# Regrouping the last expert layer of a fused transformer kernel, and the order of its row scatters

## Chip, cores and metric

The kernel runs on one core of a Trainium2 chip. The metric is device time in microseconds (us) of one execution; lower is better. A core has five engines that each work through their own queue of instructions in order: TensorE (PE) for matmuls, VectorE (DVE), ScalarE (ACT), GpSimd (POOL) and SyncE (SP), which here only issues DMAs. Engines wait for one another by semaphores. An instruction that waits also holds back whatever stands behind it in its queue.

## The reference

The input is 8 sequences of 512 tokens with 128 features. Six layers follow one another, each with a layer norm in front and a residual sum behind:

```python
x = x + 0.5 * moe(layernorm(x))    # 8 experts, each token goes to its best 2
x = x + attention(layernorm(x))    # 16 heads of 8, causal, rotary
x = x + 0.5 * moe(layernorm(x))    # same weights as the first
x = x + 0.5 * fp6(layernorm(x))    # quantized product, 128 x 128
x = x + mix(layernorm(x))          # gates, a scan along the tokens, gated FFN
x = x + 0.5 * fp6(layernorm(x))
```

An expert computes `relu(x @ W1 + b1) @ W2 + b2` with W1 of 128 x 512. The two chosen experts' outputs are weighted by a softmax over their two scores.

## The kernel before

All eight sequences X[0] to X[7] stay on chip. The layers are numbered by s: s = 0 and s = 2 are the two expert layers, s = 1 is attention, and the last three layers together are a "tail", one for each sequence.

**An expert layer** works on groups of sequences, from the table `GROUPS` (line 29): for s = 0 three and five, for s = 2 four and four. For a group, four things follow one another.

- The *front*, `moe_front` (line 330), normalizes each sequence into a tile (`um`, five buffers, for s = 2; the tiles `um` and `a0` to `a4` for s = 0) and computes the routing scores. It then finds each token's two experts and its place in a table of rows sorted by expert: the integers `at`, the gates `g1`, and the expert of each tile of rows, `eid` (lines 412 to 481). When that is done it enters the group in `groups`.
- The *scatters* (line 489) come next in the same generator: eight indirect DMAs for each sequence, issued by POOL, write its normalized rows into `rows_in[g]` in memory. So three, four and five sequences have 24, 32 and 40 scatters.
- The *tiles*, `moe_tiles` (line 498): `tiles_of(n)` = 4n + 7 tiles of 256 rows for n sequences, so 19, 23 and 27 for three, four and five. SP loads a tile's expert weights `wx` (line 511) and its rows `xs` (line 515) four tiles ahead. The load of the rows waits for all scatters of the group. PE transposes the rows (`xp`, line 525), multiplies by W1 (`hp`, line 539), ACT and DVE apply bias and relu (`hs`, lines 547 and 549), PE multiplies by W2 (`yp`, line 559), DVE adds the bias (`yo`) and SP stores to `rows_out[g]` (line 571). A tile is emitted in four pieces, each ending in a `yield`.
- The *combine*, `moe_combine` (line 595), gathers each token's two rows with indirect DMAs on POOL (`y`, line 623), eight for each sequence. DVE adds them, weighted, to X (line 614). When a sequence is through, (s, b) is in `done`.

`rows_in[g]` and `rows_out[g]` are as long as the longest group with that g needs: 23 tiles for g = 0 and 27 for g = 1. Each is cleared once at the start (line 162), ahead of the loads of the other constants on SP's queue.

**Attention** (line 639) runs through 32 units, four for each sequence. Its main loop has 212 half-steps, each a `yield`. It is emitted as a software pipeline in which the row maxima run four steps ahead of the exponentials, so its last half-steps hold exponentials and value products only.

**The tail** of a sequence (line 999) is fp6, mix, fp6 and a store: 27 short pieces, each of which crosses from one engine to another. `tails` (line 1007) keeps up to four alive; a new one may start every eight steps if its sequence is in `done`. One step of `tails` advances every live tail by one piece.

**The order of the work is written out by hand**: each engine's queue is filled in the order of emission. All parts are Python generators. `drive(main, (side, rate), ...)` (line 64) takes one step of the main generator and then `rate` steps, on average, of each side. `until(gen, ready)` runs a generator until a condition holds, checked after each `yield`; `behind` holds a generator back until a condition holds; `sent(s, g)` is true when all of a group's scatters are emitted and `filled(s, g)` when all of its tiles are stored. At the start of the program:

```python
finish(until(first_front, lambda: (0, 0) in groups))
finish(until(second_front, lambda: (0, 1) in groups))
finish(first_front)
finish(second_front)
```

The first `until` looks only when the generator yields, and the first `yield` after the entry in `groups` is the one behind the first scatter. So this order holds one scatter of the first group, then the second group's front with its first scatter, then the remaining 23 of the first group and 39 of the second.

Later, attention is the main generator (line 1055). Beside it run the remaining work of layer 0 (`early`, `tiles`, `gathering`), the front and scatters of s = 2's first group (`third`, one piece a half-step), its second group's front (`fourth`, held back until the first is sent) and the tiles of s = 2 (`beside`, held back likewise). After attention, the tiles of the first group run to their end (line 1060). Then the tiles of the second group are the main generator, with the combine of the first and the tails beside them (line 1062). At the end the remaining tails run with the combine of the second group (line 1063).

Of the kernel before, what the change touches and what calls it, by code (L numbers as in the profile page):

```python
# [25 lines left out]
NGF = 3  # L26
TW = 256

GROUPS = {0: [[0, 1, 2], [3, 4, 5, 6, 7]], 2: [[0, 1, 2, 3], [4, 5, 6, 7]]}
SIZES = sorted({len(g) for gs in GROUPS.values() for g in gs})  # L30
GTX = SIZES[-1] * NT


def tiles_of(n):

    return 2 * n * S // TW + NE - 1
# [27 lines left out]
def drive(main, *sides):  # L64

    due = [0.0] * len(sides)
    for _ in main:
        for i, (g, rate) in enumerate(sides):
            due[i] += rate
            while due[i] >= 1.0:  # L70
                due[i] -= 1.0
                next(g, None)
# [12 lines left out]
def kernel(  # L85
# [69 lines left out]
    for g in range(2):  # L155
        n = max(tiles_of(len(gs[g])) for gs in GROUPS.values()) * TW
        rows_in.append(dram.tile([n, P], F32, tag=f"rows_in{g}", name=f"rows_in{g}"))
# [140 lines left out]
    def data_from(ins, others):  # L298

        for o in others:  # L300
            tc.add_manual_dep(
                ins.ins, o.ins.name,
                mybir.DependencyInfo(mybir.DependencyClass.Sync, mybir.DependencyReason.DATA),
                reason="rows",
            )

    def unordered(ins, key):

        tc.declare_no_dep(ins.ins, group=key, reason="rows of their own")
        tc.add_to_no_dep_group(key, ins.ins)  # L310
        return ins

    def filled(s, g):
        return len(groups[s, g]["stored"]) == tiles_of(len(GROUPS[s][g]))

    def sent(s, g):
        return (s, g) in groups and len(groups[s, g]["scattered"]) == 2 * NT * len(GROUPS[s][g])

# [11 lines left out]
    def moe_front(s, g):  # L330

        name = f"{s}_{g}"
        bs = GROUPS[s][g]
        GT, NTL = len(bs) * NT, tiles_of(len(bs))
# [147 lines left out]

        scattered = []
        groups[s, g] = dict(at=at, gates=g1, eid=eid, scattered=scattered, stored=[])
        for n in range(len(bs)):
            for k in range(2):
                for t in range(NT):
                    i = n * NT + t
                    ins = nc.gpsimd.indirect_dma_start(  # L489
                        out=rows_in[g][0 : NTL * TW, :],  # L490
                        out_offset=bass.IndirectOffsetOnAxis(ap=at[:, k, i : i + 1], axis=0),
                        in_=us[n][:, t, :], in_offset=None,
                        bounds_check=NTL * TW - 1, oob_is_err=False,
                    )
                    scattered.append(unordered(ins, f"out{name}"))
                    yield

    def moe_tiles(s):

        order = [(g, i) for g in range(2) for i in range(tiles_of(len(GROUPS[s][g])))]  # L500
        T = {}
# [93 lines left out]
    def moe_combine(s, g):  # L595

        state = groups.pop((s, g))
        at, gates = state["at"], state["gates"]
        NTL = tiles_of(len(GROUPS[s][g]))
        assert len(state["stored"]) == NTL  # L600
        waiting = []

        def put():
            f, y, t, b = waiting.pop(0)
            f(y, t)
            if t == NT - 1:
                done.add((s, b))

        for n, b in enumerate(GROUPS[s][g]):

            def weighted(y, t, n=n, b=b):
                for k in range(2):
                    i = n * NT + t
                    nc.vector.scalar_tensor_tensor(
                        X[b][:, t, :], y[:, k, :], gates[:, k, i : i + 1], X[b][:, t, :],
                        ALU.mult, ALU.add,
                    )

            for t in range(NT):
                y = wk.tile([P, 2, P], F32, tag="y", name=f"y_{s}_{b}_{t}", bufs=6)  # L620
                for k in range(2):
                    i = n * NT + t
                    ins = nc.gpsimd.indirect_dma_start(  # L623
                        out=y[:, k, :], out_offset=None,
                        in_=rows_out[g][0 : NTL * TW, :],
                        in_offset=bass.IndirectOffsetOnAxis(ap=at[:, k, i : i + 1], axis=0),
                        bounds_check=NTL * TW - 1, oob_is_err=False,
                    )
                    data_from(ins, state["stored"])
                    yield  # L630
                waiting.append((weighted, y, t, b))
                if len(waiting) > 3:
                    put()
        while waiting:
            yield
            put()
# [370 lines left out]
    def tails(bs):  # L1007

        pend = list(bs)
        live = []  # L1010
        step = 8
        while pend or live:
            if pend and len(live) < 4 and step >= 8 and (2, pend[0]) in done:
                live.append(tail(pend.pop(0)))
                step = 0
            for g in list(live):
                if next(g, live) is live:
                    live.remove(g)
            step += 1
            yield  # L1020


    def behind(gen, ready):
        while not ready():
            yield
        yield from gen
# [7 lines left out]
    for s in GROUPS:  # L1034
        for g in range(2):
            fronts[s, g] = moe_front(s, g)
# [7 lines left out]
    tiles = moe_tiles(0)  # L1044
# [3 lines left out]
    early, late = moe_combine(0, 0), moe_combine(0, 1)  # L1048
    drive(until(tiles, lambda: (0, 1) in done), (early, 1.0), (fp6_weight(), 0.2))
    backlog += [early, tiles, late]  # L1050
    gathering = behind(late, lambda: filled(0, 1))
    third, fourth = fronts[2, 0], behind(fronts[2, 1], lambda: sent(2, 0))
    more_tiles = moe_tiles(2)
    beside = behind(more_tiles, lambda: sent(2, 0))
    drive(
        attention(list(range(nb)), 1),
        (early, 1.0), (tiles, 2.2), (gathering, 0.8), (third, 1.0), (fourth, 1.0), (beside, 0.9),
    )
    finish(third)
    drive(until(beside, lambda: filled(2, 0)), (fourth, 1.5))  # L1060
    rest = tails(GROUPS[2][0] + GROUPS[2][1])
    drive(beside, (fourth, 1.5), (moe_combine(2, 0), 1.0), (rest, 0.33))
    drive(rest, (moe_combine(2, 1), 2.0))


# [75 lines left out]
```

## Time and profile before

| | |
|---|---|
| median of 3 runs | 1178.27 us (1177.59 to 1180.08) |
| the profiled execution | 1177.05 us |
| its span in the profile | 1175.4 us |
| PE, DVE, ACT, POOL busy | 958.0, 688.2, 503.6, 540.3 us |
| attention's last output product (L801) begins | 749.2 us |
| first hp matmul (L539) of s = 2's second group | 818.1 us |
| last scan of a tail (L954) begins | 1133.17 us |

The profile is of one execution, with times in us from the start of the span. The page lists, for each engine, its busy time, then the span in 40 slices of 29.4 us with the busy share in tenths, and then groups of instructions: line, engine, operation, output <- input, count, busy time, mean duration in ns, and the idle time of the engine ahead of them with what ended it. The list of waits says which engine, at which line, waited for what: total, number of times, longest. The timeline has start, duration, engine, line, operation, count, and in brackets the idle time before it and its releaser. The windows give each engine's busy time within a stretch. PEld is PE's weight load, which overlaps PE. A matmul of these float32 operands shows in the trace as several passes.

### The profile page before, as it was taken

Reading aid. Unit: us, or ns where it says so; the run is one execution under the profiler, and the core shown is the slowest. Engines: PE = TensorE matmul, PEld = TensorE weight load, DVE = VectorE, ACT = ScalarE, POOL = GpSimd, SP = SyncE. Lnnn points to the kernel's source line nnn. Section 1 sums busy time; section 2 is a strip of 40 time slices with the busy share of each in tenths; the row PEclk is TensorE's granted clock in tenths of the full one; section 3 lists DMA queues with packets and bytes.
Section 4 is the critical chain, followed back from the end, with each engine's and each line's share of the span. In section 5 each row is a group of like instructions: output and inputs, shape, how many; then the busy total and the mean of one; then the engine's idle time right before and its main releaser. Section 6 shows DMA issues by size and latency. Waiting matters only on the chain.

```text
span 1175.4 us, 20511 instructions
## 1 busy us (share of the span) xinstructions
PE 958.0 (82%) x6809; PEld 654.6 (56%) x6809; DVE 688.2 (59%) x2532; ACT 503.6 (43%) x1095; POOL 540.3 (46%) x696
## 2 busy tenths in 40 slices
PE   3507997999999999999999899995969984466764
PEld 3407996777664444544445466784867852334432
DVE  7302334565567878777877563441466576777763
ACT  1302332344455655666465455331235553344441
POOL 2077707112147775433388422054572148664431
PEclk9999999999999999999999899997979995777777
DMA  9318977443200000000001422474755311100000
GB/s 290 119 50 273 272 234 220 128 143 114 73 24 26 24 24 13 1 2 2 1 31 53 140 64 84 145 228 146 232 157 164 105 32 29 33 25 10 9 9 18
DMA packets 88313, 110.07 MB, mean 94 GB/s; under 512 B 9360, under 2 KB 69648, under 8 KB 88208
## 3 DMA queue, kind: packets, MB, share of 16 engines
q1 hardware_dynamic: 80016, 91.97, 25.8%
q0 software_dynamic: 8192, 16.79, 4.7%
q8 instruction: 54, 0.88, 0.3%
q14 instruction: 51, 0.42, 0.1%
HBM read 79.63 MB, written 29.10 MB: 93 GB/s over the span
## 4 chain that ended last, share of the span: by engine, by line
PE 55%; DVE 18%; issue 11%; POOL 9%; ACT 3%; DMA 3%; POOLq 0%; SPq 0%; DVEq 0%; ACTq 0%
PE sa L705 11%; PE hp L539 9%; PE yp L559 9%; PE av L768 7%; DVE seen L722 3%; POOL y L623 3%; POOL rows_in L489 3%; PE sb L705 2%; DVE st L240 2%; PE gt L981 1%; PE tp_st L225 1%; PE lp L344 1%; PE up L982 1%; DMA rows_in<-um,at 1%; PE tp L225 1%
## 5 line engine op out<-in xcount | busy, mean ns | idle before, releaser
L722 DVE CUSTOM_DVE_ANT_0 seen<-sa,future_s 128x128 f32<-128x128 f32 (+3 forms) x512 | 224.7, 486 | 92.6 <-PE sb L705 87.6
L750 ACT ACTIVATE pm<-sb 128x512 f32<-128x512 f32 (+1 forms) x384 | 181.7, 523 | 143.6 <-PE sb L705 124.2
L547 ACT ACTIVATE hs<-hp,wx 128x256 f32<-128x256 f32 x276 | 119.9, 470 | 266.8 <-PE hp L539 254.2
L705 PE MATMUL sb<-qa,ka 32*128 32x512 f32 (+3 forms) x1024 | 210.2, 473 | 1.6 <-DVE nstat L722 1.5
L559 PE MATMUL yp<-wx,hs 128*128 128x128 f32 x1472 | 201.2, 281 | 4.8 <-ACT hs L547 3.4
L755 POOL TENSOR_SCALAR_AFFINE_SELECT pm<-pm 128x256 f32<-128x256 f32 x256 | 101.7, 411 | 220.4 <-ACT pm L750 218.0
L705 PE MATMUL sa<-ta_k,qm 32*128 32x384 f32 (+3 forms) x1024 | 200.5, 473 | 0.6 <-DVE nstat L722 0.4
L559 PEld LDWEIGHTS yp<-wx,hs 128*128 128x128 f32 x1472 | 190.4, 196 | 18.1 <-issue 6.9
L539 PE MATMUL hp<-xt,wx 128*128 128x256 f32 x736 | 197.8, 393 | 0.0
L623 POOL DMA_INDIRECT y<-rows_out,at x128 | 132.0, 1031 | 83.2 <-DMA rows_out<-yo 50.8
L549 DVE TENSOR_SCALAR hs<-hp,wx 128x256 f32<-128x256 f32 x92 | 44.4, 483 | 178.3 <-ACT hs L547 173.4
L539 PEld LDWEIGHTS hp<-xt,wx 128*128 128x128 f32 x736 | 131.0, 198 | 20.9 <-issue 5.9
L705 PEld LDWEIGHTS sa<-ta_k,qm 32*128 32x128 f32 x1024 | 91.4, 186 | 76.3 <-DVE nstat L722 20.2
L489 POOL DMA_INDIRECT rows_in<-um,at x88 | 87.1, 990 | 45.6 <-issue 19.6
L705 PEld LDWEIGHTS sb<-qa,ka 32*128 32x128 f32 x1024 | 99.7, 186 | 10.5 <-DVE nstat L722 4.2
L768 PE MATMUL av<-pm,vpad 128*32 128x512 f32 (+3 forms) x1024 | 92.3, 456 | 0.0
L525 PE MATMUL xp<-cst,xs 128*128 128x128 f32 x184 | 36.6, 282 | 60.3 <-DMA xs<-rows_in 60.3
L232 POOL TENSOR_TENSOR rs<-rs,mhalf 128x4 f32<-128x4 f32 x35 | 36.2, 1035 | 100.6 <-DVE rs L231 98.2
L527 DVE COPY xt<-xp 128x256 f32<-128x256 f32 x92 | 38.1, 414 | 54.0 <-PE xp L525 54.0
L251 ACT ACTIVATE um<-x,nb_um,rs 128x128 f32<-128x128 f32 x96 | 39.5, 482 | 67.3 <-DVE nb_um L248 59.4
L225 PE MATMUL tp_xd<-cst,q 128*128 128x128 f32 x64 | 15.1, 379 | 64.5 <-POOL q L884 64.5
L525 PEld LDWEIGHTS xp<-cst,xs 128*128 128x128 f32 x184 | 26.2, 145 | 70.9 <-issue 62.2
(190 smaller groups left out, 1367.7 us busy)
## 6 DMA issues: line engine op xcount, KB each, us to landing
wx<-in_wexp SPq DMA_DIRECT2D x92, 578.0 KB, 4.0
xs<-rows_in SPq DMA_DIRECT2D x92, 128.0 KB, 4.1
rows_out<-yo SPq DMA_DIRECT2D x92, 128.0 KB, 2.3
rows_in<-zero SPq DMA_DIRECT2D x1, 3456.0 KB, 25.3
rows_in<-zero SPq DMA_DIRECT2D x1, 2944.0 KB, 12.8
x<-in_x SPq DMA_DIRECT2D x8, 256.0 KB, 4.8
y<-rows_out,at POOLq DMA_INDIRECT x128
out_x<-x SPq DMA_DIRECT2D x8, 256.0 KB, 2.0
```

The lines of the kernel that those rows point to most:

```text
L489: ins = nc.gpsimd.indirect_dma_start(out=rows_in[g][0 : NTL * TW, :], out_offset=bass.IndirectOffsetOnAxis(ap=at[:, k, i : i + 1], axis=0) ...
L525: nc.tensor.transpose(xp[:, ts(h, P)], t["xs"][:, h, :], ident)
L539: nc.tensor.matmul(hp[:, k, :], wx[:, E_W1 + fc * P : E_W1 + (fc + 1) * P], t["xt"], start=True, stop=True,)
L547: nc.scalar.activation(hs[:, fc, :], hp[:, k, :], AF.Relu, bias=bias)
L549: nc.vector.tensor_scalar(hs[:, fc, :], hp[:, k, :], bias, 0.0, ALU.add, ALU.max)
L559: nc.tensor.matmul(yp[:, h, :], t["hs"][:, fc, ts(h, P)], wx[:, E_W2 + fc * P : E_W2 + (fc + 1) * P], start=(fc == 0), stop=(fc == NFC - 1),)
L623: ins = nc.gpsimd.indirect_dma_start(out=y[:, k, :], out_offset=None, in_=rows_out[g][0 : NTL * TW, :], in_offset=bass.IndirectOffsetOnAxi ...
L705: nc.tensor.matmul(sc[:, at : at + hi - lo], stat[rows, ts(m, P)], mov[rows, lo:hi], start=True, stop=stop,)
L722: nc.vector.tensor_tensor_reduce(out=seen(w), in0=sc[:, at : at + w], in1=future_s[:, S - w : S], scale=-1.0, scalar=3.0e38, op0=ALU.add, ...
L750: nc.scalar.activation(pm[:, h % 2, 0:w], sc[:, 0:w], AF.Exp, scale=scale)
L755: nc.gpsimd.affine_select(out=dg, in_=dg, pattern=[[0, 2], [1, P]], compare_op=ALU.is_ge, fill=0.0, base=0, channel_multiplier=-1,)
L768: nc.tensor.matmul(av[32 * j : 32 * j + 32, m * P :], Q[b]["v"][:, m * NH + NR * j + r, :], U[n]["pms"][p, j // 2][:, j % 2, at : at + S - ...
```

## The change

There are four edits. The layer s = 2 is grouped in five and three sequences. A `yield` stands between the entry in `groups` and the first scatter. The tiles of s = 2 advance beside attention at a rate of 2.0 instead of 0.9. The tails advance beside the second group's tiles at 0.6 instead of 0.33.

```diff
-GROUPS = {0: [[0, 1, 2], [3, 4, 5, 6, 7]], 2: [[0, 1, 2, 3], [4, 5, 6, 7]]}
+GROUPS = {0: [[0, 1, 2], [3, 4, 5, 6, 7]], 2: [[0, 1, 2, 3, 4], [5, 6, 7]]}
...
         groups[s, g] = dict(at=at, gates=g1, eid=eid, scattered=scattered, stored=[])
+        yield
         for n in range(len(bs)):
...
-        (early, 1.0), (tiles, 2.2), (gathering, 0.8), (third, 1.0), (fourth, 1.0), (beside, 0.9),
+        (early, 1.0), (tiles, 2.2), (gathering, 0.8), (third, 1.0), (fourth, 1.0), (beside, 2.0),
...
-    drive(beside, (fourth, 1.5), (moe_combine(2, 0), 1.0), (rest, 0.33))
+    drive(beside, (fourth, 1.5), (moe_combine(2, 0), 1.0), (rest, 0.6))
```

The lines below the new `yield` have numbers one higher in the changed kernel: the scatters of line 489 are at 490, the hp matmuls of 539 at 540. The text keeps the numbers of the kernel before. With the new groups, `rows_in[0]` has 27 tiles instead of 23, and the table of constants no longer holds a pattern for groups of four.

## The prediction

> **What bounds the kernel now.** The page comes first: its span, the slices of TensorE (PE) and the scatter row.
>
> ```profile
> span 1175.4 us, 20511 instructions
> PE   3507997999999999999999899995969984466764
> PEclk9999999999999999999999899997979995777777
> L489 POOL DMA_INDIRECT rows_in<-um,at x88 | 87.1, 990 | 45.6 <-issue 19.6
> ```
>
> One slice is 29.4 us. PE is full from slice 3 to about slice 32, so there only PE's work and the holes in it count; slices 0 to 2 and the last seven are bound by something else. Then the waits, the PE and POOL lists, name the holes (total, times, longest):
>
> ```profile
> PE tp_xd L225 <- POOL q L884: 64.5, 15, 13.8
> PE xp L525 <- DMA xs<-rows_in: 60.3, 5, 38.4
> POOL rows_in L489 <- DVE qs L463: 29.9, 1, 29.9
> ```
>
> PE waits 60.3 us for rows scattered by GpSimd (POOL). The timeline of the start shows why the longest of those is 38.4 us:
>
> ```profile
> 25.87 1.21 POOL L489 DMA_INDIRECT rows_in<-um,at  x1 [4.60 <-DVE q L461]
> 57.02 0.99 POOL L489 DMA_INDIRECT rows_in<-a,at  x1 [29.95 <-DVE qs L463]
> 86.55 0.98 POOL L489 DMA_INDIRECT rows_in<-um,at  x1 [0.30 <-issue]
> 87.83 0.98 POOL L489 DMA_INDIRECT rows_in<-a,at  x1 [0.30 <-issue]
> 88.81 0.38 SPq L515 DMA_DIRECT2D xs<-rows_in  x1
> 91.13 0.66 PE L525 MATMUL xp<-cst,xs 128*128 128x128 f32 x2 [38.39 <-DMA xs<-rows_in]
> ```
>
> One scatter of the first group (um) goes at 25.87. The next in POOL's queue is one of the second group (a), whose places are ready only at 57. The other 23 of the first group stand behind it, though their places are known since 25.87. A second hole lies late, before the tiles of the last layer's second group:
>
> ```profile
> 801.06 1.03 PE L539 MATMUL hp<-xt,wx 128*128 128x256 f32 x4
> 811.26 0.97 POOL L489 DMA_INDIRECT rows_in<-um,at  x1 [0.30 <-issue]
> 815.94 0.66 PE L525 MATMUL xp<-cst,xs 128*128 128x128 f32 x2 [13.85 <-DMA xs<-rows_in]
> ```
>
> The windows compare the stages (length, then busy PE, PEld, DVE, ACT, POOL; clock; DMA share; GB/s):
>
> ```profile
> 708.00:740.00 32.00, 30.19 (x245) 19.85 (x244) 10.70 (x45) 15.65 (x35) 7.59 (x17) 1.00 0.19 59
> 818.00:846.00 28.00, 28.00 (x193) 25.99 (x193) 10.85 (x34) 9.18 (x21) 12.18 (x13) 0.98 0.83 256
> 1004.00:1046.00 42.00, 23.37 (x101) 14.77 (x100) 32.45 (x95) 14.85 (x34) 29.84 (x28) 0.76 0.12 32
> 1050.00:1106.00 56.00, 39.75 (x144) 24.85 (x145) 40.48 (x130) 27.50 (x60) 25.22 (x23) 0.70 0.03 10
> ```
>
> The end of attention and the tiles alone fill PE. Where only tails run (the last two), VectorE (DVE) is the fullest, at 77% and 72%, and no engine is full: chains of short steps across engines set the pace.
>
> **What the Trainium skill says.** "DMA: Bandwidth & Descriptors", section on the anatomy of a DMA on the GpSimd path: each has a fixed cost of about 2 us. The trace agrees: scatters land 2.25 us after issue. "SBUF — State Buffer", section "SBUF: two separate sides": GpSimd can't write descriptors while a DVE operation holds the shared port. This matters because the first group's scatters will now run beside the routing of the second. The trace shows little of it: from 830 to 850, beside a half-busy DVE (9.71 of 20 us), gathers keep a spacing of 1.30 us, against 1.28 for scatters with DVE idle at 60 to 87. "TensorE: Matmul & The Clock Gate", section "Part 1: The HAM clock gate": after some 3.4 us of idleness PE starts at half clock. The trace agrees: after the 13.85 us hole eight yp matmuls take 1.92 us, later 1.05.
>
> **The change, part by part.**
>
> *The yield before the scatters.* POOL's order becomes 24 scatters of the first group, then 40 of the second. The places are there at 25.87. The clear that comes before grows from 2944 KB (12.8 us, issued at 7.68) to 3456 KB; in proportion 15.0 us, landing at 22.7, so still hidden. The constants lose the pattern for four sequences, an eighth of that load; at most 0.3 us, counted as nothing. The 24th scatter issues at 25.87 + 23 x 1.283 = 55.4, where now the last is at 86.55: **-31.1 us**. The steps that follow it (SP issue, load, first xp, 4.6 us) stay. The second group's 40 start at about 57 instead of 87.8 and so keep the same lead over its tiles. POOL, SP and PE all move together, up to the third layer's front. Bounds: -25 if descriptors are delayed by DVE (it is busy 11.5 us from 27 to 91; half of it), -32 at best.
>
> *Groups of five and three; rate 2.0 beside attention.* Before, about 9.5 tiles of the first group ran beside attention (38 of its 92 hp matmuls in program order, four to a tile). In the changed order, 40 scatters follow the fifth sequence at one per attention step, and the first xp stands after the last transpose of attention. So none runs inside attention; 4.5 precede the last sequence's y, but behind all of attention's scores. The rate of 2.0 has almost nothing to act on. PE's work is only moved, since PE is full there. Built up from PE's times:
> - y of the sixth sequence: 639.29 - 31.1 = 608.2.
> - The next y, with the same matmuls as from 590.12 to 639.29 and no tiles: +49.2 = 657.4.
> - The last stretch without tiles: attention's PE work from 708 to 740 is 9.5 + 5.6 + 2.6 us, and 3 for its chain of exponentials and copies: +20.7 = 678.
> - A new wait. Six scatters stand after the last mask: 6 x 1.28 + 2.25 landing + 3.6 to xp = 13.5 us, less some 4.5 of value matmuls: +9. First fill of the tile pipeline, as from 91.13 to 95.23: +4. Together 691. Now this start costs only 2.20 + 2.84 us. Bounds for both items together 5 to 20.
> - 27 tiles at 3.73 us (xp at 821.15, the next at 824.88): 100.7. The last y, three fronts with um transposes and scores, and the routing's matmuls: 8.5. Together **800**, against 818 now.
>
> The 13.85 us hole goes: the fronts of three need about 25 us after the last sequence (749 to 771.4 now, for the routing), then 24 scatters x 1.28 = 31, plus 5. They are through some 62 us after the tiles start, and are needed after about 95.
>
> *Five tails beside the tiles of three, rate 0.6.* All tails advance by one step at a time. By the loops' counts, 30 such steps are emitted before the last tile now and 60 after it; changed, 45 and 52 (PE's order agrees: 12 of 64 fp6 product matmuls before the last tile now, 24 changed). Steps with a live tail beside tiles: 26, becoming 37; sums of live tails over steps 56 and 160, becoming 93 and 123.
>
> Beside tiles: the first tail step runs at 850.9, 32 us after 818.3, because 16 gathers come first on POOL (829 on, 1.3 each). With the store queue not held up by the hole I take 28. From 850 to 960 it is 110/26 = 4.23 us a step, of which PE work is about 3.8: three quarter-tiles of 0.93, and 26 us of tail matmuls over 26 steps (11 groups of transposes at 0.6, 3 products at 0.9, 16 gate matmuls at 0.86, one output at 2.7, in program order before the last tile; changed 16, 6, 30 and 2, so 46). It is PE-bound. Changed, a step holds 1.67 quarter-tiles, 1.55 us, and more tails: PE work is (56 + 46)/37 = 2.8 us. So chains decide, not PE. Tails alone take 3.5 us a step with three live (1049.65 to 1077.41, eight steps between two scans); a tile's share of DVE adds about 0.5 (1.3 us a tile for xt, hs and yo, 0.42 tiles a step). With the gathers, and one or two live, 3.3 to 3.9. I take 8 steps at 3.4, 8 at 3.9, 8 at 4.0, 13 at 4.2: 144 us, 3.9 a step. Bounds 3.3 (122) to 4.7 (174). 800 + 28 + 144 = 972, against 960 now for the end of the tiles.
>
> Tails alone afterwards: 12 steps with gathers at 4.6 (now 4.3 to 4.9 from 967.8 to 1049.7), 25 at 3.3, 15 at the end at 2.8 (1133.2 to 1175.4 now): 55 + 82 + 42 = 179, against 215 now. Bounds 167 to 192. End: 972 + 179 = 1151; 1.65 us lie outside the span (1177.05 - 1175.4), which makes 1152.7 in that execution's time. The median is 1.2 above it: about 1153.
>
> **Rivals.**
> - *The overlap is better than I take it* (chance 0.2): tail steps beside tiles at 3.3 us and 167 for the rest. 122 + 28 + 167 + 800 = 1117, about 1120; halfway to it, 1136. For it: no engine is full in such steps. Against it: the order is fixed, and PE's 64.5 us of waits for POOL's q products show what one late step does to every tile behind it.
> - *The tails hold up the tiles* (0.09; ends slower): at 0.6 a step's transposes reach PE before DVE and POOL have made their input, and the tiles stand behind. Break-even is 1178 - 1153 = 25 us, or 3.9 + 25/37 = 4.6 us a step. At 5.2, with 192 for the rest, it ends at about 1153 + 48 + 13 = 1214; just beyond the turning point, 1181. For it: 4.85 us a step with three tails and gathers, from 967.8 to 1006.6. Against it: there two gathers go to a step, and later none.
> - *The start brings less* (0.08): scatters beside the clears and constant loads that run until 40 us land late. "DMA: Bandwidth & Descriptors", section "Queues, rings and completion order", has each DMA engine take turns between queues, and at 91 to 138, under a DMA share of 0.83, scatters keep 1.28 us. It would give 1160 to 1172.
>
> That the change doesn't do what it says holds for the part beside attention; it is in my forecast.
>
> **How the numbers follow.** The forecast as worked out has 0.63: **1153 us**, own range 1136 to 1172. Half of the better-overlap case lies below that, so the low end goes to 1128; the high end is 1174, short of most of the slower rival. Less than 0.2% (2.4 us) could not be told from no change here. Faster: 0.63 + 0.20 + 0.07 = 0.90; same 0.02; slower 0.08.
>
> **What would show it.** First xp near 60 us, and the POOL wait of 29.9 us gone. No L539 inside attention; an xp wait of some 9 us near 680 in place of the 13.85. The second group's first L539 near 800, the last tile near 972, then about 179 us. The forecast is wrong if xp at the start stays beyond 75, if PE waits on tp_xd grow by more than 40 us, or if a new xp wait of over 20 us stands at the end of attention.

## The result, and the profile after

| | before | changed |
|---|---|---|
| median | 1178.33 us (4 runs) | 1158.38 us (4 runs, 1156.0 to 1160.64) |
| ratio of the times, 95% interval | | 0.9828 [0.9803, 0.9854] |
| the profiled execution, its span | 1177.05, 1175.4 us | 1156.0, 1154.3 us |
| first xp | 91.13 | 60.40 us |
| yo of the last tile of s = 2's first group | 826.32 | 807.47 us |
| yo of the last tile of all | 961.17 | 978.51 us |
| from there to the end | 214.2 | 175.8 us |

The change makes the kernel 20 us faster. The page of the changed kernel, with its slices now of 28.9 us:

```profile
span 1154.3 us, 20541 instructions
PE   3589978999999999999999949999777787645774
PEclk9999998999999999999999979999888899767776
```

PE's slice 2 holds an 8 where it held a 0, and its first 9 comes one slice earlier. A new dent (the 4) stands in slice 23, at the end of attention, and slices 28 to 31, where tiles and tails share PE, hold sevens. PE's waits:

```profile
PE tp_xd L225 <- POOL q L885: 51.3, 15, 11.6
PE tp_xf L225 <- ACT xf L972: 28.8, 6, 9.3
PE xp L526 <- DMA xs<-rows_in: 21.4, 4, 8.1
```

The wait for rows fell from 60.3 to 21.4 us; the waits of the tails' transposes (tp_xd and tp_xf) hardly changed in sum, 80.1 us after 83.2. The timeline of the start (start, duration, engine, line, operation):

```profile
26.06 1.21 POOL L490 DMA_INDIRECT rows_in<-um,at  x1 [4.60 <-DVE q L461]
27.58 0.98 POOL L490 DMA_INDIRECT rows_in<-um,at  x1 [0.31 <-issue]
...
55.67 0.97 POOL L490 DMA_INDIRECT rows_in<-um,at  x1 [0.30 <-issue]
57.45 0.97 POOL L490 DMA_INDIRECT rows_in<-a,at  x1 [0.81 <-issue]
...
58.06 0.38 SPq L516 DMA_DIRECT2D xs<-rows_in  x1
...
60.40 0.66 PE L526 MATMUL xp<-cst,xs 128*128 128x128 f32 x2 [7.42 <-DMA xs<-rows_in]
```

The 24 scatters of the first group follow one another, the last at 55.67 where it stood at 86.55. They keep 1.29 us apiece beside the second group's routing on DVE. The end of attention:

```profile
679.28 1.11 PE L225 MATMUL tp_avt<-cst,avs 128*128 128x128 f32 x4 [0.76 <-ACT avs L777]
...
688.53 0.66 PE L526 MATMUL xp<-cst,xs 128*128 128x128 f32 x2 [8.14 <-DMA xs<-rows_in]
```

The first tile of s = 2 comes after attention's last transpose, and PE waits 8.14 us for its rows. The hole of 13.85 us before the second group's tiles is gone. The windows of what follows (length, busy PE, PEld, DVE, ACT, POOL, clock, DMA share, GB/s), tiles alone and then tiles with tails:

```profile
803.40:831.00 27.60, 23.89 (x166) 22.06 (x164) 10.79 (x37) 7.41 (x17) 15.35 (x16) 0.99 0.81 244
831.00:978.50 147.50, 111.97 (x590) 87.56 (x590) 101.17 (x305) 65.01 (x147) 71.31 (x66) 0.85 0.25 72
```

In the second window PE is busy 76% of the time, DVE 69% and POOL 48%: nothing is full.

### The profile page after: what moved, and what is told of

It reads as the page before. It is cut to its first block, busy times and chain, and to the rows that moved or that the text cites. A ratio compares the mean times of both kernels' runs of the same rounds, so it can differ in the third digit from the quotient of the medians.

```text
span 1154.3 us, 20541 instructions
## 1 busy us (share of the span) xinstructions
PE 959.7 (83%) x6809; PEld 658.0 (57%) x6809; DVE 690.7 (60%) x2532; ACT 502.6 (44%) x1095; POOL 540.3 (47%) x696
## 4 chain that ended last, share of the span: by engine, by line
PE 60%; DVE 20%; POOL 6%; issue 5%; ACT 5%; DMA 3%; SPq 0%; POOLq 0%; DVEq 0%; ACTq 0%
PE hp L540 12%; PE yp L560 11%; PE sa L706 11%; PE av L769 7%; DVE seen L723 4%; POOL y L624 2%; PE sb L706 2%; DVE st L240 2%; DMA y<-rows_out,at 2%; PE xp L526 1%; PE lp L344 1%; PE tp_st L225 1%; PE gt L982 1%; PE tp L225 1%; PE yp L914 1%
## 5 line engine op out<-in xcount | busy, mean ns | idle before, releaser
L769 PEld LDWEIGHTS av<-pm,vpad 128*32 128x32 f32 x1024 | 23.8, 109 | 76.9 <-POOL pm L756 39.0
L615 DVE SCALAR_TENSOR_TENSOR x<-y,g,x 128x128 f32<-128x128 f32 x128 | 55.6, 436 | 11.2 <-DMA y<-rows_out,at 9.1
L526 PE MATMUL xp<-cst,xs 128*128 128x128 f32 x184 | 37.5, 288 | 21.4 <-DMA xs<-rows_in 21.4
```

The costliest lines, as they stand in the source:

```text
L526: nc.tensor.transpose(xp[:, ts(h, P)], t["xs"][:, h, :], ident)
L615: nc.vector.scalar_tensor_tensor(X[b][:, t, :], y[:, k, :], gates[:, k, i : i + 1], X[b][:, t, :], ALU.mult, ALU.add,)
L769: nc.tensor.matmul(av[32 * j : 32 * j + 32, m * P :], Q[b]["v"][:, m * NH + NR * j + r, :], U[n]["pms"][p, j // 2][:, j % 2, at : at + S - ...
```

## The experiments

My theory: the `yield` alone brings 31 us. The other three edits together cost some 11: the grouping removes one hole and opens another, the rate of 2.0 has nothing to act on, and the rate of 0.6 makes the tiles wait for the tails. The rival: the grouping and the rates bring the gain, as their description suggests.

**The yield alone**, in the kernel before:

```diff
         groups[s, g] = dict(at=at, gates=g1, eid=eid, scattered=scattered, stored=[])
+        yield
```

> The kernel before with the yield before the scatters and nothing else. My theory: the first rows reach PE 31 us earlier and everything behind keeps its distances, so the 13.9 us hole before the second group's tiles of the last layer is still there and the time is 1178 - 31 = 1147 us, about 11 us below the whole change. Rival, that the grouping and the rates bring the gain: 1170 to 1178.

Measured: 1152.5 us, ratio 0.9782 [0.9762, 0.9803]. One line gives 25 us, more than the whole change. Two xp lines of its timeline:

```profile
628.86 0.66 PE L526 MATMUL xp<-cst,xs 128*128 128x128 f32 x2 [5.75 <-DMA xs<-rows_in]
...
791.70 0.66 PE L526 MATMUL xp<-cst,xs 128*128 128x128 f32 x2 [13.85 <-DMA xs<-rows_in]
```

The hole is exactly as before. The wait at the first tile within attention is 5.75 us where it was 2.20. The rival falls.

The first xp is 30.6 us earlier, the end of the span 24. Five of the missing us go between the output products of the sixth and the seventh sequence, 73.2 us apart where it was 68.1: PE waits 8.7 us for rows instead of 5.0, and the same 548 matmuls keep it busy for 63.6 us instead of 62.3. The cause is the same line. The `yield` stands in the last layer's generators too, and moves their scatters one half-step back: the last of the first group's 32 now has 220 of attention's masks ahead of it on POOL, where it had 218, while the first row transpose has 864 value matmuls ahead of it on PE in both.

**The change without the yield.**

```diff
         groups[s, g] = dict(at=at, gates=g1, eid=eid, scattered=scattered, stored=[])
-        yield
```

> The changed kernel without the yield: groups of five and three, rates 2.0 and 0.6. My theory: 31 us more than the changed kernel, 1158 + 31 = 1189 us, so the other three edits together cost 11 us against the kernel before. Rival, that they bring something by themselves: below 1176.

Measured: 1188.24 us, ratio 1.0086 [1.0066, 1.0106]: 29.9 us above the changed kernel, and slower than the kernel before. First xp is at 90.91. So the other three edits, by themselves, lose 10 us. Beside the yield they lose 6 (1158.38 against 1152.5).

**The tail rate back to 0.33**, all else as changed.

```diff
-    drive(beside, (fourth, 1.5), (moe_combine(2, 0), 1.0), (rest, 0.6))
+    drive(beside, (fourth, 1.5), (moe_combine(2, 0), 1.0), (rest, 0.33))
```

> The changed kernel with the tails beside the last tiles at the old rate of 0.33. My theory: beside tiles a tail step then costs 4.2 us and is limited by PE, 21 steps with a live tail instead of 37, so the last tile comes at about 803 + 28 + 88 = 919 us; the 63 steps behind it take about 224 us. End 1143 in the span, 1147 us: 11 us faster than the change. Rival, that 0.6 is what pays for the grouping: 1165 to 1190.

Measured: 1144.2 us, ratio 0.9713 [0.9691, 0.9735]: 14.2 us faster than the change. The last tile's yo is at 918.95, where 919 was expected. Its window of tiles with tails:

```profile
831.00:919.00 88.00, 72.65 (x432) 60.85 (x431) 53.80 (x165) 38.02 (x86) 46.20 (x44) 0.92 0.41 124
```

Beside tiles PE is now 83% busy, against 76% at 0.6. From the first group's last yo to the end it takes 333.0 us, the change 346.8 and the kernel before 349.1. The kernel before has four tiles more there, 14.9 us; taken off, 334.2. So the grouping costs nothing in these stages and the rate of 0.6 costs 14 us. How, the whole way from the second group's first hp to the end shows, first at 0.6 and then at 0.33:

```profile
803.40:1154.30 350.90, 236.44 (x1132) 170.34 (x1130) 224.08 (x683) 134.21 (x298) 171.46 (x160) 0.80 0.20 59
```

```profile
805.80:1142.90 337.10, 234.00 (x1132) 166.27 (x1130) 222.87 (x683) 135.95 (x298) 171.62 (x160) 0.81 0.21 62
```

PE has the same 1132 matmul records in both. At 0.6 it is idle for 114.5 us and at 0.33 for 103.1; its busy time differs by 2.4 us only. So the loss is waiting. While tiles and tails run together, PE waits at the tails' transposes for 30.6 of 147.5 us at 0.6 and for 10.6 of 88.0 at 0.33, and the tiles stand behind them in its queue.

Set against the yield alone (1152.5 us), this kernel is 8.3 us faster. So with the yield in place the grouping does gain something, and the tail rate takes more than that back. The rate of 2.0, which it keeps, does nothing, as the next run shows. PE's waits for rows in the last layer fit: 22.5 us with the yield alone (at the first tiles and in the hole), 11.9 us here.

**The tile rate back to 0.9 beside attention**, all else as changed.

```diff
-        (..., (beside, 2.0),
+        (..., (beside, 0.9),
```

> The changed kernel with the tiles of the last layer at the old rate of 0.9 beside attention. My theory: no tile stands inside attention in either, because the scatters are only through at its end, so within 4 us of the changed kernel (1154 to 1162). Rival, that the rate of 2.0 does bring tiles beside attention and saves time there: 1165 or more.

Measured: 1160.31 us, ratio 0.9846 [0.9826, 0.9867], 1.9 us from the changed kernel. The first row transpose waits as there, at the same place:

```profile
690.61 0.66 PE L526 MATMUL xp<-cst,xs 128*128 128x128 f32 x2 [9.16 <-DMA xs<-rows_in]
```

The rate is without weight with these groups: the first group's scatters are not all through before attention's last transposes.

**Four kernels on a slower chip.** The next four were compared on another chip, where the kernel before took 1253 us instead of 1178. In their traces PE stands idle ahead of the products with the expert weights (of the run with groups of four and the tile rate of 0.5, 50.2 us in ten waits ahead of yp, to which the profile gives no releaser). Their times can't be set against the others; two of them were run again elsewhere, below. Two results stand. First, tiles really beside attention:

```diff
-        (..., (third, 1.0), (fourth, 1.0), (beside, 2.0),
+        (..., (third, 2.0), (fourth, 1.0), (beside, 2.0),
...
-    drive(beside, (fourth, 1.5), (moe_combine(2, 0), 1.0), (rest, 0.6))
+    drive(beside, (fourth, 1.5), (moe_combine(2, 0), 1.0), (rest, 0.33))
```

> Groups of five and three, the yield, tails at 0.33, tiles at 2.0 beside attention, and the first group's front and scatters at 2.0 pieces a half-step, so that 15 tiles do stand inside attention and 20 before its last output product. My theory: that saves the 11 us of waits for rows at attention's end and about 5 us of stalls there, but leaves only 6.5 tiles (24 us) to cover the second group's routing and 24 scatters (58 us): a new hole of about 33 us, so 1144 - 13 + 33 = 1164 us. Rival, that tiles beside attention save time as the change meant: below 1140.

Measured: 1293.04 us beside 1253.07, ratio 1.0333 [1.0295, 1.0371]. The hole that was expected opens late, since too few tiles are left to cover the second group's routing and scatters:

```profile
937.07 0.66 PE L526 MATMUL xp<-cst,xs 128*128 128x128 f32 x2 [26.57 <-DMA xs<-rows_in]
```

It explains only part of the loss; the rest is that of the run with the tile rate of 0.9, told below. Second, groups of four and four with the yield and tails at 0.6:

```diff
-    drive(beside, (fourth, 1.5), (moe_combine(2, 0), 1.0), (rest, 0.33))
+    drive(beside, (fourth, 1.5), (moe_combine(2, 0), 1.0), (rest, 0.6))
```

> Groups of four and four, the yield, tiles at 0.9, and the tails beside the second group's tiles at 0.6 instead of 0.33. My theory: 51 steps with a live tail beside the tiles at 3.9 us each instead of 26 at 4.2, and 60 steps behind them with fewer live tails at about 2.9: 798 + 28 + 199 + 174 = 1199 us. Rival, that the rate of 0.6 harms only with groups of five and three: 1153 us or less.

Measured: 1276.98 us, ratio 1.0198 [1.0176, 1.0221]. It can be set only against the run of groups of four on the same chip (1241.39 us, the next one): 35.6 us, in which two edits differ. The traces part them: up to the last yo of the first group, where of the two edits only the tile rate acts, the difference is 14.3 us (889.47 against 875.14). From there to the end it is 29.6, with PE as long busy on the same 1208 matmul records (250.7 and 251.6 us), so all of it is waiting. The two profiled executions lie 5.3 us above and 3.1 below their medians, so I estimate that the tail rate costs between 21 and 30 us there: less than the 46 that I expected, but not only with groups of five and three, as the rival has it.

**Groups of four, the yield, fewer tiles beside attention.** The opposite of what the change meant to do, in the kernel with the yield alone:

```diff
-        (..., (beside, 0.9),
+        (..., (beside, 0.5),
```

> Groups of four and four, the yield, tails at 0.33, and the tiles of the last layer slowed from 0.9 to 0.5 beside attention. My theory: PE is full in attention, so a tile moved out of it costs nothing; four more tiles (15 us) then stand behind attention and fill the 13.9 us hole in which PE waits for the second group's 32 scatters. 1152.5 - 13.9 = 1139 us. Rival, that tiles beside attention are hidden there and each one moved out costs its 3.7 us: 1152 to 1154.

On the slower chip: 1241.39 us, ratio 0.9915 [0.9898, 0.9932]. Run again:

> The kernel with groups of four and four, the yield, tiles at 0.5 beside attention and tails at 0.33 once more, since the kernel before took 1253 us in its first comparison instead of 1178, with PE waiting for weights. My theory, where the kernel before takes about 1178: the 13.9 us hole is filled by four more tiles behind attention, 1152.5 - 13.9 = 1139 us. Rival: a tile moved out of attention costs its 3.7 us, 1152 to 1154.

Measured: 1128.62 us, ratio 0.9577 [0.9562, 0.9591], the fastest of all: 23.9 us below the yield alone, 29.8 below the change. The expectation had the cause right and was 10 us short. One window for each, from the sixth sequence's output product to the end of the first group's tiles, first with the rate of 0.9 and the yield alone:

```profile
608.40:802.30 193.90, 166.44 (x1270) 124.00 (x1267) 83.05 (x322) 78.26 (x175) 67.01 (x98) 0.93 0.42 129
```

and then with the rate of 0.5:

```profile
610.10:779.70 169.60, 161.23 (x1270) 120.71 (x1267) 81.81 (x321) 78.45 (x175) 66.91 (x99) 0.97 0.47 147
```

The same 1270 matmul records take 24.3 us less. PE's idle time falls by 19.1 us: the hole of 13.85, and the wait at the first tile, 5.75 to 0.31 us, since at the lower rate the row transposes stand further back in PE's queue, the first behind 872 value matmuls instead of 864. PE's busy time falls by another 5.2 us, as the clock rises from 0.93 to 0.97. So the rival, that a tile moved out of attention costs its own time, falls: PE is full on both sides of that border.

**Five and three, with the front at double pace and tiles at 0.9.**

```diff
-        (..., (third, 1.0), (fourth, 1.0), (beside, 2.0),
+        (..., (third, 2.0), (fourth, 1.0), (beside, 0.9),
...
-    drive(beside, (fourth, 1.5), (moe_combine(2, 0), 1.0), (rest, 0.6))
+    drive(beside, (fourth, 1.5), (moe_combine(2, 0), 1.0), (rest, 0.33))
```

> As the run with front and tiles both at 2.0, but the tiles at 0.9: 7 inside attention, 9.5 before its last output product, 17.5 (65 us) behind it. My theory: the waits at attention's end go and no hole opens, 1144 - 12 = 1132 us. Rival, that those waits are only replaced by equal ones inside attention: 1142 to 1146.

On the slower chip: 1287.53 us, ratio 1.0287 [1.0265, 1.0308]. Run again:

> The kernel with groups of five and three, front at 2.0, tiles at 0.9 beside attention and tails at 0.33 once more, for the same reason. My theory: 1144 - 12 = 1132 us, since 7 tiles fill the stalls at attention's end. Rival, that the waits for rows there are only replaced by equal ones inside attention: 1142 to 1146. A third way, which the first trace suggests (PE waited 13.4 us for rows inside attention): the front at double pace and its scatters hold attention up, 1150 or more.

Measured: 1183.71 us (ten runs, 1178.4 to 1190.7), ratio 1.0052 [1.0027, 1.0077]. My theory was wrong by 52 us here; the third way holds, in both its parts. The run with tails at 0.33 (1144.2 us) has the front at a rate of 1.0. The windows from the first sequence's output product to the fifth's, ahead of every scatter of the layer, first with the front at 2.0 and then with 1.0:

```profile
338.60:569.20 230.60, 217.25 (x1844) 108.04 (x1840) 167.16 (x701) 129.24 (x273) 110.41 (x189) 0.92 0.03 10
```

```profile
339.70:553.50 213.80, 205.50 (x1844) 101.48 (x1840) 166.63 (x701) 129.60 (x273) 110.09 (x189) 0.98 0.04 10
```

So 17 us are lost by the front alone, for the same 1844 matmul records. PE waits four times, 8.3 us in all, for normalized rows (um) that ACT has not made yet, and its clock is lower.

The rest is lost with the scatters: two of them a half-step are too many for POOL. Its queue in attention then:

```profile
642.08 0.99 POOL L490 DMA_INDIRECT rows_in<-um,at  x1 [0.17 <-issue]
643.37 0.97 POOL L490 DMA_INDIRECT rows_in<-um,at  x1 [0.30 <-issue]
644.35 0.43 POOL L756 TENSOR_SCALAR_AFFINE_SELECT pm<-pm 128x256 f32<-128x256 f32 x1
```

No gap here is longer than 0.3 us. Attention's masks (pm) stand between the scatters, and its value matmuls wait for the masks (total, times, longest):

```profile
PE av L769 <- POOL pm L756: 12.7, 5, 3.6
```

The window from the first scatter to where PE begins to wait for rows, and one of the run with tails at 0.33, where one scatter goes to a half-step:

```profile
611.00:668.00 57.00, 43.66 (x362) 22.02 (x358) 28.59 (x121) 22.71 (x46) 48.52 (x64) 0.85 0.16 51
```

```profile
611.00:654.60 43.60, 40.99 (x432) 21.37 (x429) 32.81 (x142) 26.49 (x57) 38.32 (x58) 1.00 0.15 48
```

PE is 77% busy where it was 94%. POOL, with 85% and 88% and the short gaps behind its scatters, is nearly full in both. At one scatter a half-step it still keeps up with attention, at two it sets the pace.

## Why the prediction was right

The step list and what the changed kernel's trace shows, in us:

| step | predicted | measured |
|---|---|---|
| first xp | 60 | 60.40 |
| y of the sixth sequence, of the next | 608.2, 657.4 | 613.15, 656.79 |
| attention's last transposes | 678 | 679.28 |
| wait of the first xp there | 9 | 8.14 (then 2.97) |
| second group's first hp | 800 | 803.41 |
| from there to the first tail step | 28 | 28.3 |
| steps with a live tail beside tiles, each | 3.9 | 3.97 |
| last tile | 972 | 978.5 |
| tails alone | 179 | 175.8 |
| end of the span | 1151 | 1154.3 |
| median | 1153 | 1158.4 |

- *The yield* brought 30.7 us at the first xp; the larger clear stayed hidden (the first scatter is at 26.06 instead of 25.87), and DVE didn't slow the scatters. The run with the yield alone keeps 24 of these 31 us at the end of its span. I had not priced that the same `yield` delays the last layer's scatters by a half-step.
- *The groups and the rate of 2.0*: no tile of s = 2 inside attention, a new wait, the old hole gone, all as stated. The run at 0.9 shows that the rate does nothing. That this part came out is in part luck: the sixth sequence's y is 5 us later than forecast and the way from it to the next is 5.6 us shorter, so that two errors cancel.
- *The tails*: the two stages came out 3 us late and 3 us early, which cancel as well. The rival of a better overlap did not come, nor did the tails hold the tiles up to its turning point of 4.6 us a step. But the prediction's sum hid what the run at 0.33 shows: of the two rates, 0.6 is the worse by 14 us. The prediction set the new groups with the new rate against the kernel before, and never against the new groups with the old rate.
- *A slip*: the prediction and the table of before call the hp at 818.1 the second group's first. It is the first group's last; the second group's is at 822.26. The way to the first tail step is then 28.6 us before and 28.3 after: unchanged, so my reason for taking 28 instead of 32, the store queue, is not shown. A second slip is in the rival of the start: from 91 to 138 the DMA share is 0.92, not 0.83, which makes its point stronger.
- *The size*: of the 5 us between forecast and median, 3.3 lie in the span and 1.2 in the distance of the profiled execution from the median, 2.4 us where I took 1.2. The remaining 0.9 is my rounding: 1152.7 and 1.2 make 1153.9. The four terms of the steps beside tiles, likewise, add up to 145, not 144.

## What to carry to other kernels

A condition that is looked at only when a generator yields takes effect one piece late; here that put one waiting scatter ahead of 23 ready ones in an in-order queue, and the one line that moves it back was worth more than the whole change. Where one engine is full, moving its work from one stage into another gains nothing by itself; keep as much of it as covers the next group's wait, and ask of each rate which queue must carry it. Price each edit of a change alone: here the yield gained 25 us, the grouping beside it another 8, and the tail rate took 14 back.

## What the runs showed of the hardware

A wait on PE can cost more than its length. Between the rates of 0.9 and 0.5, 19.1 us less idle time came with 5.2 us less busy time for the same matmuls. "TensorE: Matmul & The Clock Gate", section "Part 1: The HAM clock gate", gives a reason in the Trainium skill: PE falls to half clock after some 3.4 us without work. The granted clock of 0.93 against 0.97 agrees. So does the stretch behind the hole in the run with the yield alone: from 791.7 to 795.0 the clock is 0.50 with PE busy all the time, and from 795.2 to 802.3 it is 1.00. That this accounts for all of the 5.2 us is not shown, and I did not separate it from other causes. The front at double pace points the same way: there 5.1 us more idle time came with 11.7 us more busy time for the same matmuls, at 0.92 against 0.98.

The kernel with the tile rate of 0.5 took 1241 us on one chip and 1129 on another. In its first tiles, on the slower chip and then on the other:

```profile
69.00:185.00 116.00, 72.01 (x435) 64.16 (x434) 25.44 (x74) 22.23 (x51) 45.91 (x51) 0.81 0.45 141
```

```profile
60.00:176.00 116.00, 103.86 (x683) 95.21 (x683) 38.89 (x114) 35.71 (x83) 69.46 (x76) 0.98 0.81 252
```

In the same 116 us the slower one moves 141 GB/s instead of 252, and PE does 435 of the 683 matmuls. Why, and whether it lies in the chip itself, no run here tells.
